# A mixture-of-experts routing table kept by expert and rank, written while tokens are still being counted

## The chip, the core and the metric

The kernel runs on one core of one Trainium2 chip. The metric is the device time of one execution in microseconds. A core has TensorE (PE), VectorE (DVE), ScalarE (ACT), GpSimd (POOL) and SyncE (SP), which run side by side, each through its own list of instructions in order. SP and POOL also issue DMA transfers; the indirect ones (rows picked by a list of indices) are POOL's.

## What is computed

8192 tokens of 512 numbers are first modulated per batch (a product with a 512x512 matrix), then go through a shared expert and through 8 of 64 routed experts, and the sum is added to the input. Cut to what matters here:

```python
x, cond_512: (8, 1024, 512), (8, 256)
y = clip(((x * styles) @ weight.T) * dcoefs + bias, -256, 256)        # 8192 tokens
shared = silu(y @ sh_gate_w) * (y @ sh_up_w) @ sh_down_w               # hidden width 1024
scores = sigmoid(y @ router_w.T); sb = scores + e_bias                 # 64 experts in 8 groups of 8
# the 4 groups with the largest sum of their two best sb stay; of them the 8 best experts
topk_idx = top_k(where(in 4 groups, sb, -inf), 8); w = scores[topk_idx] / (sum + 1e-20)
order = argsort(topk_idx.reshape(-1), stable=True)                     # 65536 (token, expert) pairs
tok = order // 8
o = (silu(y[tok] @ gate_w[e]) * (y[tok] @ up_w[e])) @ down_w[e]        # expert of each pair, width 256
routed[tok] += o * w
out = x + shared + routed
```

How many tokens an expert gets depends on the data.

## The kernel before

All products are made from high and low halves of the float32 numbers, three matmuls for each.

*Stage one* (to about 244 us) goes over 16 tiles of 512 tokens: load_x brings a tile of x on SP, split_x makes its halves (ACT xh, DVE xl), cond multiplies on PE, cond_out and cond_lo make y, its halves, its transposed copy for DRAM (y_d by rows, yT_d by columns), logits and scores make the router's scores. early_masks makes the first MA = 2 of eight masks meanwhile: route_mask(c) marks, for chunk c of 1024 tokens, the 8 chosen experts of every token, on DVE alone.

*Stage two* (to about 1343 us) is the shared expert: 128 steps, 8 for each tile of 512 tokens. A step is gate_up (24 matmuls), hidden (ACT, DVE, ACT, DVE) and the down products of the step before (12 matmuls), about 8.2 us. The order of PE, ACT, DVE and SP is written out by hand. Between the steps runs the generator route_slots, which makes the routing table on DVE. Each step has a credit of DVE time (the last lines of the loop) and takes pieces of the generator until the credit is used; HOP ends the step's share, because a matmul that was put into the list "later" has to run first, behind the next gate_up.

The table (tokw) says for every block of 128 places which token and which weight each place has. A block belongs to one expert; blocks are processed in units of one, two or four, of which there are fixed numbers (64, 64, 85, and up to 15 more of four, in groups that are skipped if not wanted). Before: the remaining masks, sums per chunk (r8), totals per expert, the layout of units, and then for each chunk ranks and slots (count, raise_), the eight largest (V.max), their scores (q, w8), the weights, and the address ad. Then POOL writes the chunk's 8 x 8 columns of 128 pairs (token, weight), 8 bytes a pair, with 64 indirect transfers to the table's copy in DRAM, tab_d; every burst of 8 of them waits until the burst before has landed. After the last chunk one transfer reads tab_d back to tokw.

At step 124 the first weights and the first gathers of *stage three* are put into the order, and from step 126 its first transposes; stage three goes over the 213 units: gather of rows of y_d by tokw (POOL), turn_x (PE), halves (ACT xh, DVE xl), gate and up (part, half), down_c, weigh, and scatter, an indirect transfer that adds to out (POOL). Its order comes from plan and arrange, a small scheduler at build time.

Of the kernel before, what the change touches and what calls it, by code (L numbers as in the profile page):

```python
# [21 lines left out]
P = 128  # L22
B, L, C = 8, 1024, 512
N = B * L
# [39 lines left out]
def body(ctx, tc, xT, x, condT, wT, vecs, affT, rwT, ebias, wexp, shgu, shdn, cst, out):  # L64
# [12 lines left out]
    tab_d = nc.dram_tensor("tab_d", [P * NSB, 2], I32).ap()  # L77
# [8 lines left out]
    tokw = pp.tile([P, NSB, 2], I32, name="tokw")  # L86
# [64 lines left out]
    MA = 2  # L151
    GUA = (1, 2, 13)
    rank0 = rp.tile([P, NBC, G, G], F32, name="rank0")
    V.memset(rank0, 0.0)
# [49 lines left out]
    with ExitStack() as actx:  # L204
# [167 lines left out]

        with tc.manual_schedule(engines={ET.PE, ET.Activation, ET.DVE}):
# [20 lines left out]
            for j in range(1, NT):  # L394
# [3 lines left out]
                if j in GUA:  # L398
                    fetch_gu(GUA.index(j), xa, 1)
                for m in range(KC):  # L400
                    cond_to(j, m)
                    for k in range(KC):
                        cond(j, m, k)
                    for k in ((0,), (1,), (), (2, 3))[m] if more else ():
                        split_x(j + 1, k)
                    cond_out(j, m)
                    cond_lo(j - (m == 0), (m - 1) % KC)
                    if m == 1 and j >= 2:
                        scores(j - 2)
                    elif j >= 3 and m % 2 == 0:  # L410
                        next(mgen, None)
# [71 lines left out]
    def gather(u, s, g):  # L483
        queued(GP.indirect_dma_start(xg[g % RXG].bitcast(F32), None, y_d, IOA(tokw[:, u.block + s, 0:1], 0)))  # L484
# [49 lines left out]
    def weigh(u, s, d):  # L534
        S.mul(oc[d % ROC], po[d % 2], tokw[:, u.block + s, 1:2].bitcast(F32))  # L535

    def scatter(u, s, d):
        i_ = queued(GP.indirect_dma_start(out, IOA(tokw[:, u.block + s, 0:1], 0), oc[d % ROC], None, compute_op=ALU.add))  # L538
# [205 lines left out]
    with ExitStack() as bctx:  # L744
# [19 lines left out]
        def route_slots():  # L764

            for c in range(MA, NB // NBC):
                for cost in route_mask(c):
                    yield cost  # L770

            for c in range(NB // NBC):
                V.tensor_reduce(r8[:, :, c], mask[:, c].bitcast(F32), axis=AX.X, op=ALU.add)
                yield 0.8
            rs = sbt.tile([P, E, NB // NBC], F32R, name="rs", tag="d2")
            V.tensor_tensor_scan(rs.rearrange("p e c -> p (e c)"), rst, r8.rearrange("p e c -> p (e c)"), 0.0, ALU.mult, ALU.add)
            ps = psr.tile([P, 512], F32, name="ps")
            later.append(lambda: PE.matmul(ps, lhsT=oner, rhs=rs.rearrange("p e c -> p (e c)"), start=True, stop=True))
            yield HOP
            base = sbt.tile([P, E, NB // NBC], F32, name="base", tag="dd")  # L780
            V.tensor_copy(base, ps.rearrange("p (e c) -> p e c", e=E))


            ecnt = sbt.tile([E, 12], F32, name="ecnt")
            eci = sbt.tile([E, 4], I32, name="eci")
            ed = sbt.tile([E, E], F32, name="ed")
            V.tensor_tensor(ed, base[:E, :, NB // NBC - 1], ident[:E, :E], ALU.mult)
# [18 lines left out]
            tb = sbt.tile([P, 2, 8], I32, name="tb")  # L806
            gp = sbt.tile([P, 8], F32, name="gp")
            gs = sbt.tile([P, 8], F32, name="gs")
# [11 lines left out]
            off = 0  # L820
            for b in range(TBITS - 1, -1, -1):
                V.tensor_scalar(tbit[:, b:b + 1], ti[:, 5:6], b, 1, ALU.logical_shift_right, ALU.bitwise_and)
                V.tensor_scalar(tb[:, 0, b:b + 1], ti[:, 5:6], b + 1, b + 1, ALU.logical_shift_right, ALU.logical_shift_left)
                V.tensor_scalar(tb[:, 1, b:b + 1], tb[:, 0, b:b + 1], -4.0, 4.0 * off, ALU.mult, ALU.add)
                off += 1 << b
            yield 1.5
            V.tensor_copy(gp[:, :TBITS], tb[:, 0, :TBITS])
            V.tensor_tensor(gs[:, :TBITS], tb[:, 1, :TBITS], tbit[:, :TBITS], ALU.mult)
# [13 lines left out]

            dg = sbt.tile([E, 5, E], F32, name="dg", tag="d2")
            e6 = sbt.tile([E, 8], F32, name="e6")
            V.tensor_scalar(e6[:, 1:2], ecnt[:, 4:5], float(P), None, ALU.mult)
            V.scalar_tensor_tensor(e6[:, 0:1], ecnt[:, 1:2], -float(QT), e6[:, 1:2], ALU.mult, ALU.add)
            V.scalar_tensor_tensor(e6[:, 2:3], ecnt[:, 2:3], -2.0, ecnt[:, 5:6], ALU.mult, ALU.add)
            V.scalar_tensor_tensor(e6[:, 2:3], e6[:, 2:3], float(P), e6[:, 1:2], ALU.mult, ALU.subtract)
            V.scalar_tensor_tensor(e6[:, 3:4], ecnt[:, 2:3], 2.0 * P, e6[:, 1:2], ALU.mult, ALU.add)
            V.tensor_tensor(e6[:, 4:5], ecnt[:, 6:7], ecnt[:, 3:4], ALU.subtract)  # L850
            V.tensor_tensor(e6[:, 4:5], e6[:, 4:5], ecnt[:, 5:6], ALU.subtract)
            V.tensor_scalar(e6[:, 4:5], e6[:, 4:5], float(P), None, ALU.mult)
            for q in range(5):
                V.tensor_scalar(dg[:, q], ident[:E, :E], e6[:, q:q + 1], None, ALU.mult)
            later.append(lambda: PE.matmul(ps[:, 192:192 + 5 * E], lhsT=ones[:E], rhs=dg.rearrange("p a e -> p (a e)"), start=True, stop=True))

            def count(c):
                so = sbt.tile([P, E, 8], F32R, name="so", tag="d2")
                V.tensor_tensor_scan(so.rearrange("p e b -> p (e b)"), rst, mask[:, c].rearrange("p e b -> p (e b)").bitcast(F32), 0.0, ALU.mult, ALU.add)

                def over():
                    PE.matmul(ps, lhsT=oner, rhs=so.rearrange("p e b -> p (e b)"), start=True, stop=False)
                    PE.matmul(ps, lhsT=trir, rhs=mask[:, c].rearrange("p e b -> p (e b)"), start=False, stop=True)

                later.append(over)

            def raise_(c):
                sc = rp.tile([P, E, 8], F32, name="sc", tag="sb")
                V.tensor_tensor(sc, ps.rearrange("p (e b) -> p e b", b=8), first[:, :, c:c + 1].to_broadcast([P, E, 8]), ALU.add)  # L873
                yield 0.8

                dd = sbt.tile([P, E, 8], F32, name="dd")
                d2 = sbt.tile([P, E, 8], F32, name="d2")
                for d_, o_ in ((dd, 1), (d2, 3)):
                    V.tensor_tensor(d_, sc, odd[:, o_].unsqueeze(2).to_broadcast([P, E, 8]), ALU.is_gt)
                    V.tensor_tensor(d_, d_, odd[:, o_ + 1].unsqueeze(2).to_broadcast([P, E, 8]), ALU.mult)  # L880
                    yield 1.5
                V.tensor_tensor(dd, dd, d2, ALU.add)
                V.tensor_tensor(sc, sc, dd, ALU.add)
                V.tensor_tensor(sc, sc, mask[:, c].bitcast(F32), ALU.mult)
                yield 2.1
                return sc

            yield HOP
            odd = sbt.tile([P, 5, E], F32, name="odd")
            V.tensor_copy(odd, ps[:, 192:192 + 5 * E].rearrange("p (a e) -> p a e", e=E))  # L890
            first = sbt.tile([P, E, NB // NBC], F32, name="first")
            V.tensor_copy(first[:, :, 0], odd[:, 0])
            V.tensor_tensor(first[:, :, 1:], base[:, :, :-1], odd[:, 0].unsqueeze(2).to_broadcast([P, E, NB // NBC - 1]), ALU.add)
            count(0)
            yield HOP

            def owners():

                ic = sbt.tile([E, NE], F32, name="ic", tag="d2")
                for o, blk in ((0, cs[:E, C_IOTA:C_GRP]), (NE - NX, ex)):  # L900
                    q = ic[:, o:o + blk.shape[-1]]
                    V.tensor_scalar(q, blk, ecnt[:, 4:5], None, ALU.is_ge)
                    V.scalar_tensor_tensor(q, blk, ecnt[:, 5:6], q, ALU.is_ge, ALU.add)
                    V.scalar_tensor_tensor(q, blk, ecnt[:, 6:7], q, ALU.is_ge, ALU.add)
                later.append(lambda: PE.matmul(ps[:1, 192:192 + NE], lhsT=ones[:E, 0:1], rhs=ic, start=True, stop=True))
                yield HOP
                ie = sbt.tile([1, 2, NE], F32, name="ie", tag="dd")
                V.tensor_scalar(ie[:, 0], ps[:1, 192:192 + NE], E - 0.5, -float(E), ALU.is_gt, ALU.mult)
                V.tensor_tensor(ie[:, 1], ie[:, 0], ps[:1, 192:192 + NE], ALU.add)
                V.tensor_scalar(ie[:, 0], ie[:, 1], E - 0.5, -float(E), ALU.is_gt, ALU.mult)  # L910
                V.tensor_tensor(ie[:, 1], ie[:, 0], ie[:, 1], ALU.add)
                V.tensor_scalar(iexp, ie[:, 1], float(E - 1), None, ALU.min)
                yield 1.5
# [3 lines left out]
            for c in range(NB // 8):  # L917
# [3 lines left out]
                if c == 1:  # L921
                    yield from owners()
# [252 lines left out]
```

## Time and profile before

| what | value |
|---|---|
| median of 3 runs | 3781.26 us (3776.44 to 3785.31) |
| profiled execution, its own time | 3782.01 us |
| its span, from the first to the last instruction | 3780.1 us |
| PE, DVE, ACT, POOL busy | 98%, 59%, 50%, 55% of the span |
| mean granted PE clock | 0.995 |
| table writes tab_d (L967), POOL | 512, mean 1045 ns |
| gathers xg (L484) and scatters out (L538), POOL | 532 each, mean 1121 and 1785 ns |

A profile row gives the start and the length of an instruction in microseconds, its engine, its line in the kernel and the tiles that it writes and reads; in brackets stands how long its engine was idle before it, and what ended that. Matmuls overlap, so their lengths add up to more than the time that they take; the distance of their starts says how fast they follow each other. SPq and POOLq are the engines' issuing parts.

### The profile page before, as it was taken

How to read it: one execution, taken by the hardware profiler on the slowest of the kernel's cores; microseconds unless marked ns; L12 is line 12 of the kernel's file. 1: busy time of each engine (PE TensorE's matmuls, PEld its weight loads, DVE VectorE, ACT ScalarE, POOL GpSimd, SP SyncE). 2: the span in 40 equal slices, each digit the busy share in tenths (PEclk: the TensorE clock that was granted, in tenths of full speed). 3: DMA queues.
4: the chain of work that ended last, by engine and by line, in shares of the span. 5: the costliest groups of instructions: out<-in, count | busy, mean ns of one | idle time of the engine just before them, and what ended most of it. 6: DMA issues, size and time to landing. Idle time of an engine off the chain costs nothing.

```text
span 3780.1 us, 53475 instructions
## 1 busy us (share of the span) xinstructions
PE 3720.7 (98%) x19009; PEld 3116.9 (82%) x19009; DVE 2240.5 (59%) x3429; ACT 1883.2 (50%) x2883; POOL 2089.8 (55%) x1588
## 2 busy tenths in 40 slices
PE   9999999999999899999999999999999999999998
PEld 7777778888888778888888888888888888888886
DVE  6778765666532255566656565656665656665654
ACT  6552111111111156666666666666666666666664
POOL 0000056666666656666666666666665666666663
PEclk9999999999999999999999999999999999999999
DMA  7751111112111277787776766776766676666664
GB/s 246 211 167 60 48 51 51 52 37 65 35 51 51 77 196 168 151 208 178 162 167 146 167 133 140 157 137 129 161 130 127 137 133 116 138 112 118 115 118 65
DMA packets 233333, 464.13 MB, mean 123 GB/s; under 512 B 42464, under 2 KB 75232, under 8 KB 227296
## 3 DMA queue, kind: packets, MB, share of 16 engines
q0 software_dynamic: 135696, 280.15, 40.2%
q1 hardware_dynamic: 96368, 179.40, 15.1%
q8 instruction: 152, 2.49, 0.3%
q14 instruction: 125, 1.02, 0.1%
q10 hardware_dynamic: 992, 1.06, 0.1%
HBM read 532.75 MB, written 191.97 MB: 192 GB/s over the span
## 4 chain that ended last, share of the span: by engine, by line
PE 83%; DVE 5%; POOL 5%; issue 3%; DMA 3%; ACT 1%; SPq 0%; POOLq 0%; DVEq 0%; ACTq 0%
PE pg L511 35%; PE po L531 20%; PE gu L116 11%; PE po L1017 5%; PE pg L520 5%; POOL tab_d L967 4%; PE pt L488 4%; PE py L305 2%; DMA tab_d<-tokw,ad 1%; DVE e L196 0%; DVE yl L69 0%; DMA yT_d<-yf 0%; PE pg L525 0%; DMA xr<-in_xT 0%; PE plt L330 0%
## 5 line engine op out<-in xcount | busy, mean ns | idle before, releaser
L538 POOL DMA_INDIRECT out<-oc,tokw x532 | 949.9, 1785 | 564.4 <-ACT oc L535 243.7
L967 POOL DMA_INDIRECT tab_d<-tokw,ad x512 | 534.9, 1045 | 742.0 <-DVE sc L873 451.1
L511 PE MATMUL pg<-xh,gh 128*128 128x512 f32 (+1 forms) x2384 | 834.1, 350 | 0.0
L511 PE MATMUL pg<-xh,gl 128*128 128x512 f32 (+1 forms) x2384 | 823.5, 345 | 0.0
L511 PE MATMUL pg<-xl,gh 128*128 128x512 f32 (+1 forms) x2384 | 820.8, 344 | 0.0
L484 POOL DMA_INDIRECT xg<-y_d,tokw x532 | 596.5, 1121 | 345.1 <-PE pt L488 194.9
L69 DVE TENSOR_TENSOR gl<-wg,gh 128x1024 fp32r<-128x1024 f32 x426 | 520.1, 1223 | 109.3 <-ACT gh L499 96.9
L511 PEld LDWEIGHTS pg<-xh,gl 128*128 128x128 f32 x2384 | 449.7, 189 | 57.1
L511 PEld LDWEIGHTS pg<-xl,gh 128*128 128x128 f32 x2384 | 449.8, 189 | 55.6
L511 PEld LDWEIGHTS pg<-xh,gh 128*128 128x128 f32 x2384 | 449.8, 189 | 53.1
L499 ACT CAST gh<-wg 128x1024 fp32r<-128x1024 f32 x426 | 448.1, 1055 | 0.7 <-DMA wg<-in_wexp 0.7
L535 ACT ACTIVATE oc<-po,tokw 128x512 f32<-128x512 f32 x532 | 369.5, 695 | 153.7 <-PE po L531 138.1
L69 DVE TENSOR_TENSOR xl<-pt,xh 128x512 fp32r<-128x512 f32 x532 | 357.0, 687 | 149.2 <-ACT xh L491 107.5
L531 PE MATMUL po<-dh,hh 128*128 128x512 f32 x1064 | 427.0, 401 | 1.0 <-ACT hh L660 1.0
L531 PE MATMUL po<-dh,hl 128*128 128x512 f32 x1064 | 418.4, 393 | 0.4 <-DVE hl L69 0.4
L531 PE MATMUL po<-dl,hh 128*128 128x512 f32 x1064 | 416.0, 391 | 0.0
L116 PE MATMUL gu<-yl,guh 128*128 128x512 f32 x1024 | 404.9, 395 | 4.4 <-DVE yl L69 4.4
L116 PE MATMUL gu<-yh,guh 128*128 128x512 f32 x1024 | 402.8, 393 | 3.9 <-ACT yh L72 3.9
L658 DVE TENSOR_TENSOR hf<-hf,pg 128x512 f32<-128x512 f32 x170 | 117.0, 688 | 481.4 <-PE pg L511 477.0
L116 PE MATMUL gu<-yh,gul 128*128 128x512 f32 x1024 | 401.5, 392 | 0.0
L491 ACT CAST xh<-pt 128x512 fp32r<-128x512 f32 x532 | 301.4, 587 | 189.4 <-PE pt L488 80.0
L69 DVE TENSOR_TENSOR dl<-wd,dh 128x1024 fp32r<-128x1024 f32 x213 | 260.6, 1224 | 89.4 <-ACT dh L499 72.9
(239 smaller groups left out, 5632.4 us busy)
## 6 DMA issues: line engine op xcount, KB each, us to landing
wg<-in_wexp SPq DMA_DIRECT2D x213, 1024.0 KB
wd<-in_wexp SPq DMA_DIRECT2D x213, 512.0 KB
y_d<-yt SPq DMA_DIRECT2D x64, 256.0 KB
xn<-in_x SPq DMA_DIRECT2D x64, 256.0 KB
out<-xn SPq DMA_DIRECT2D x64, 256.0 KB
xr<-in_xT SPq DMA_DIRECT2D x60, 256.0 KB
yT_d<-yf SPq DMA_DIRECT2D x60, 256.0 KB
yr<-yT_d SPq DMA_DIRECT2D x60, 256.0 KB
```

What stands on the lines that cost most here:

```text
L69: V.tensor_tensor(o, a, b, ALU.subtract)
L116: PE.matmul(p_, lhsT=w_[:, q * KC + k], rhs=y_[k], start=n == 0, stop=n == 3 * KC - 1)
L484: queued(GP.indirect_dma_start(xg[g % RXG].bitcast(F32), None, y_d, IOA(tokw[:, u.block + s, 0:1], 0)))
L491: S.copy(xh[u.xq][:, :, s * P:(s + 1) * P], pt_of(g).bitcast(F32))
L499: S.copy(a[u.q][:, sl], (wg, wg, wd)[c][u.kind][:, sl])
L511: PE.matmul(out, lhsT=w_[u.q][:, c:c + P], rhs=x_[u.xq][:, k, :w], start=n == 0, stop=n == 3 * KC - 1)
L520: PE.matmul(out.rearrange("p (o h) -> p o h", o=2), lhsT=x_[u.xq][:, k, :P], rhs=wv[:, k], start=n == 0 and i == 0, stop=n == 5 and i == 1)
L531: PE.matmul(po[d % 2], lhsT=h_[u.q][:, k, s * P:(s + 1) * P], rhs=w_[u.q][:, k * C:(k + 1) * C], start=n == 0, stop=n == 5)
L535: S.mul(oc[d % ROC], po[d % 2], tokw[:, u.block + s, 1:2].bitcast(F32))
L538: i_ = queued(GP.indirect_dma_start(out, IOA(tokw[:, u.block + s, 0:1], 0), oc[d % ROC], None, compute_op=ALU.add))
L967: i_ = GP.indirect_dma_start(tab_d, IOA(ad[:, b, k:k + 1], 0), tw[:, b, k], None)
L1017: PE.matmul(acc[j][s], lhsT=h_[:, ts], rhs=w_[c], start=c == 0 and n == 0, stop=c == HC - 1 and n == 2)
```

## The change

The table in DRAM gets a place for every expert and rank: 64 rows of 128 places for each of 64 experts, and four rows that stay empty. A pair's place is then expert x 8192 + rank, which needs no totals, so each chunk is written as soon as its mask and running counts are there. After the last chunk the totals are made, the layout of units follows as before, and for each of the 592 blocks the row of tab_d that belongs to it is computed. Five indirect reads fetch these rows (up to 128 of 1 KB each), and PE turns them into tokw (token and weight now lie in two halves of it). MA is 1. The credit is 2.7 in all steps. The empty table is written in four parts of 1 MB during tiles 3 to 6 of stage one. The generator waits, when the reads are issued, until step 118.

```diff
-    tab_d = nc.dram_tensor("tab_d", [P * NSB, 2], I32).ap()
+    NR = N // P
+    tab_d = nc.dram_tensor("tab_d", [E * NR + 4, 2 * P], F32).ap()
+    places = tab_d.rearrange("r (s w) -> (r s) w", w=2)
...
-    tokw = pp.tile([P, NSB, 2], I32, name="tokw")
+    tokw = pp.tile([P, 2 * NSB], F32, name="tokw")
+    slot_tok, slot_w = tokw[:, :NSB].bitcast(I32), tokw[:, NSB:]
...
-    MA = 2
+    MA = 1
...
+        pat = tokw[:, :2 * N * K // P]
+        tok = pat.rearrange("p (s w) -> p w s", w=2)[:, 0]
+        GP.memset(pat, 0.0)
+        GP.iota(tok.bitcast(I32), pattern=[[1, N * K // P]], base=N, channel_multiplier=0)
+        ini = wa.tile([P, 256], I32, name="ini")
+        GP.iota(ini[:, :P], pattern=[[1, P]], base=0, channel_multiplier=0)
...
+        def constants():
+            V.tensor_copy(tok, tok.bitcast(I32))
+            V.tensor_copy(ebase, ini[:, P:P + E])
+            V.tensor_copy(erow, ini[:E, 200:201])
+            V.tensor_copy(block, ini[:, :P])
...
+        def clear(r):
+            SP.dma_start(
+                tab_d[:E * NR].rearrange("(p r f) w -> p r (f w)", p=P, f=4)[:, 2 * r:2 * r + 2],
+                pat.unsqueeze(1).to_broadcast([P, 2, 8 * P]),
+            )
+            if r == 0:
+                SP.dma_start(tab_d[E * NR:].rearrange("(a r) w -> a (r w)", a=1), pat[0:1])
...
+                if j == 2:
+                    V.tensor_copy(tok, tok.bitcast(I32))
+                if 3 <= j < 7:
+                    clear(j - 3)
+                if j == 8:
+                    GP.iota(tok.bitcast(I32).rearrange("p (b k) -> p b k", k=K), pattern=[[P, NB], [0, K]], base=0, channel_multiplier=1)
+                if j == 10:
+                    constants()
...
 route_slots:
-            for c in range(MA, NB // NBC):
-                for cost in route_mask(c):
-                    yield cost
             for c in range(NB // NBC):
-                V.tensor_reduce(r8[:, :, c], mask[:, c].bitcast(F32), axis=AX.X, op=ALU.add)
-                yield 0.8
...
+                if c >= MA:
+                    yield from route_mask(c)
+                so = sbt.tile([P, E, 8], F32R, name="so")
+                d1 = sbt.tile([P, E, 8], F32, name="d1")
+                S.copy(d1, mask[:, c].bitcast(F32))
+                if c:
+                    V.tensor_tensor(d1[:, :, 0], d1[:, :, 0], upto.bitcast(F32), ALU.add)
+                V.tensor_tensor_scan(so.rearrange("p e b -> p (e b)"), rst, d1.rearrange("p e b -> p (e b)"), 0.0, ALU.mult, ALU.add)
+                upto = sbt.tile([P, E], F32R, name="upto", bufs=2)
+                V.tensor_copy(upto, so[:, :, 7].bitcast(F32))
+                def over():
+                    PE.matmul(ps, lhsT=oner, rhs=so.rearrange("p e b -> p (e b)"), start=True, stop=False)
+                    PE.matmul(ps, lhsT=trir, rhs=mask[:, c].rearrange("p e b -> p (e b)"), start=False, stop=True)
+                later.append(over)
+                yield HOP
+                sc = rp.tile([P, E, 8], F32, name="sc", tag="sb")
+                V.tensor_tensor(sc, ps.rearrange("p (e b) -> p e b", b=8), ebase.unsqueeze(2).to_broadcast([P, E, 8]), ALU.add)
+                V.tensor_tensor(sc, sc, mask[:, c].bitcast(F32), ALU.mult)
...
+                V.tensor_scalar(ad, p8, -1.0, None, ALU.add)
...
-                        i_ = GP.indirect_dma_start(tab_d, IOA(ad[:, b, k:k + 1], 0), tw[:, b, k], None)
+                        i_ = GP.indirect_dma_start(places, IOA(ad[:, b, k:k + 1], 0), tw[:, b, k], None)
...
-            GP.dma_start(tokw, tab_d.rearrange("(p s) w -> p s w", p=P))
...
+            for g in range(0, NSB, P):
...
+                inn = sbt.tile([E, 3, P], F32, name="inn", tag="so")
...
+                def row(inn=inn, n=n, g=g // P):
+                    for r in range(3):
+                        PE.matmul(ps[:n, g:g + 1], lhsT=inn[:, r, :n], rhs=ones[:E, 0:1], start=r == 0, stop=r == 2)
+                later.append(row)
+                yield HOP
...
+            for g in range(NG):
+                n = min(P, NSB - g * P)
+                GP.indirect_dma_start(tg[g][:n], None, tab_d, IOA(rows_[:n, g:g + 1], 0))
+            while len(holding):
+                yield HOP
+            for dst, w in ((slot_tok, 0), (slot_w, 1)):
+                for a in range(0, NG, 4):
...
+                            PE.transpose(ps[:, (g - a) * P:(g - a) * P + n], tg[g][:n].rearrange("b (s w) -> b w s", w=2)[:, w], ident[:n, :n])
+                    later.append(turn)
+                    yield HOP
+                    V.tensor_copy(dst[:, a * P:a * P + w_], ps[:, :w_])
...
-        SP.dma_start(tab_d.rearrange("(p s) w -> p s w", p=P), tini)
...
+                if i == len(steps) - 10:
+                    holding.clear()
-                credit = min(credit, 0.0) + (0.0 if not i else 2.5 if writing else 3.4 if i < HC else 5.5)
+                credit = min(credit, 0.0) + (0.0 if not i else 2.7)
```

The removed lines that are not shown are raise_, owners, the 320-column broadcast of five numbers per expert (dg, L843 to L855) and the search for a slot's group (L951 to L958).

## The prediction

> **What bounds the kernel now.** The page comes first: its busy shares, then the slices, then the stretches of the windows view around every slice in which the PE is not full.
>
> ```profile
> PE 3720.7 (98%) x19009; PEld 3116.9 (82%) x19009; DVE 2240.5 (59%) x3429; ACT 1883.2 (50%) x2883; POOL 2089.8 (55%) x1588
> PE   9999999999999899999999999999999999999998
> ...
> POOL 0000056666666656666666666666665666666663
> ```
>
> The PE is the bound: 3720.7 of 3780.1 us, so at most 59 us of it are idle time. An edit gains only where it removes such idle time (or a lowered clock), and every PE instruction that it adds in stage two is paid in full. The one weak slice in the middle is the 14th. The windows view (us, busy time and count by engine, clock, DMA share, GB/s) shows stage two as full and one hole:
>
> ```profile
> 900.00:1000.00 100.00, 100.00 (x439) 82.14 (x438) 58.97 (x102) 19.00 (x32) 63.66 (x61) 1.00 0.18 49
> 1200.00:1300.00 100.00, 100.00 (x438) 81.93 (x438) 24.27 (x37) 16.82 (x28) 65.32 (x66) 1.00 0.15 43
> 1300.00:1400.00 100.00, 86.23 (x445) 71.38 (x444) 47.49 (x60) 44.23 (x66) 52.70 (x45) 0.95 0.66 197
> ```
>
> The POOL and PE timelines tell what the hole is (start, length, what, and in brackets the idle time before it and its releaser):
>
> ```profile
> 483.21 1.46 POOL L967 DMA_INDIRECT tab_d<-tokw,ad  x1 [451.12 <-DVE sc L873]
> ...
> 1308.05 0.96 POOL L967 DMA_INDIRECT tab_d<-tokw,ad  x1 [0.31 <-issue]
> 1310.77 0.58 POOL L979 DMA_DIRECT2D tokw<-tab_d  x1 [1.76 <-DMA tab_d<-tokw,ad]
> 1319.57 1.01 POOL L484 DMA_INDIRECT xg<-y_d,tokw  x1 [8.22 <-DMA tokw<-tab_d]
> ...
> 1325.51 0.72 PE L488 MATMUL pt<-idr,xg 128*128 128x128 f32 x4 [12.06 <-DMA xg<-y_d,tokw]
> ```
>
> The 512 table writes hold POOL from 483 to 1309 us. The table is read back by 1319, the first gather lands at 1325.4, and the transposes that PE has in its order since 1313.45 wait 12.06 us. The time is set by when writing begins (483, at the end of step 24 of 128) and by its pace. The rest of the idle time stands in the PE's waits of two other stretches:
>
> ```profile
> PE py L305 <- DVE xl L289: 6.5, 6, 1.4
> PE py L305 <- ACT xh L288: 4.1, 4, 1.6
> ...
> 390.93 0.79 PE L116 MATMUL gu<-yl,guh 128*128 128x512 f32 x1 [3.29 <-DVE yl L69]
> 391.52 0.63 PE L116 MATMUL gu<-yh,gul 128*128 128x512 f32 x1
> ```
>
> The first two lines are stage one (60 to 240 us). At 390.93 the PE starts a tile of the shared expert late, because DVE is still in masks; and a wait has a second price: the next matmuls start 0.43 us apart instead of 0.23 until 397.0, 14 of them, 2.8 us more. The same holds at 318.93 (3.61 us of waiting for yh) and, shorter, after 1325.5.
>
> **The change part by part.**
>
> *Writing begins earlier.* A chunk's addresses no longer need all eight masks, the totals and the blocks. Counting out the new order of DVE's instructions by step gives addresses at the ends of steps 9, 21, 33, ... 93: twelve steps of about 8.2 us, 98 us a chunk. In before step 9 lies at about 335 us; with what is lost ahead of it I take 340. The pace of POOL: 512 writes from 483.2 to 1309 are 825 us, 1.61 each (mean 1.045 of generating, 0.30 of issue, and once in eight about 2.4 us of waiting for the burst before to land: (136.0 + 13)/63). 103 us a chunk is slower than DVE's 98, so POOL keeps the pace: the last write at 340 + 825 = 1165, landed at 1167. The blocks' rows are ready at step 103 (about 1120), the five reads of 1 KB rows stand behind the writes on POOL (and the gathers behind them), are issued at 1.0 us each and landed by about 1176. PE's transposes of them come at step 119, which the PE reaches at about 1256. The spare time is 89 us, 1.4 us for each of 63 burst waits.
>
> So the wait at 1313 goes: 12.06 us, and the slow matmuls after it (six at 0.43 for 0.23, and the first transposes 0.72 for 0.46: 1.4). What is late next: the second transposes need the one pt buffer back, behind h, hh, gh, gl, xl on ACT and DVE. The same chain one step later took 4.4 us from the end of a gate_up and left PE 1.16 us idle; here 1.3. Net -12.2. The gathers, now free from step 122 (about 1285), have 28 us for the 5.8 us that one took.
>
> *A rule against it.* Row first: a write took 962 ns at the median and 1877 at most, and the rate is 61 in 100 us beside a DVE at 59% and 66 beside one at 24%. The Trainium skill, SBUF — State Buffer, section Who interferes with whom, says that DVE in a two-port mode and GpSimd shut each other out for a whole instruction, and tensor_scalar is one that can enter it. The change moves seven masks under the writes. By the rule each of its 0.64 us tensor_scalars could hold a write up, 5 us or so in all with the small ones; by the row the whole spread between busy and idle DVE is 8%, some 65 us if I took it all. Both fit into 89 us; I take 0 on the path.
>
> *The writes' places.* Neighbouring ranks of an expert were 592 x 8 B apart, and are now 8 B apart. No row of before shows landing times for that. Low end: a little faster, worth nothing, for POOL is off the path then. High end: the Trainium skill, DMA: Bandwidth & Descriptors, Specifications, says that under 512 B an SDMA engine reads, modifies and writes, and its Latency section gives 0.8 us as the least round trip to HBM. If the 16 or so neighbours of a burst (1024 places over 64 experts) had to take turns, that would be 13 us a burst for 2.4, an estimate: 63 x 10.6 - 89, a sum of +570. The 2.4 us row is nearest (the same 8 B writes by the same queue); I take 2.4 to 2.9 and no cost, and keep the high end as a rival.
>
> *DVE at the start of stage two.* Credit per step falls from 5.5 to 2.7 in steps 8 to 22. Steps 14 and 15 carry about 7 us of DVE work for 8.2 us of PE, so yl is in time at 390: -3.3 - 2.8 = -6.1. The wait at 318 stays: it hangs on the last dnl of step 6 (a buffer that SP needs for yr), behind DVE's routing work, 4.3 us in before and two triples q, q, w in after, 2 x (1.14 + 0.69 + 0.69) = 5.0: +0.8. The small waits at 463 to 486 (1.8 in all): -0.8.
>
> *PE's own work.* Added: five groups of three 64x128 f32 matmuls with one column. The nearest row, L799 (two passes, 0.31 us with its weight loads), gives 3 x 0.31 + 0.1 = 1.0 a group: 5.0. Ten f32 transposes at 0.12 (L525: two in 0.24) with four gaps of 0.15: 1.8. Removed: the 320-column broadcast L855 (423.56 to 424.38, 0.82), and L778 becomes shorter (0.1). The counting matmuls stay eight pairs. Net +5.9, between 4 and 7. DVE's new block work (steps 94 to 103) and the eight copies of masks on ACT (17 to 20% busy) lie beside a full PE; without that cover they would cost 15 and 5 us.
>
> *Stage one.* SP gets four clears of 1 MB and one row of 4 KB; the old 592 KB clear goes. 30 us at 312 to 314 GB/s make 3.3 us a clear; the share of the DMA engines is 0.70 to 0.80 from 75 to 135 us, where they fall, and would be 0.95. Behind each clear on SP stand y_d, yT_d and the next xr, for which split_x, and then PE, wait. But SP itself waits for yt at that place (30.5 us in 10 waits), which takes most of a clear. Bounds 0 and 13 (all four), I take +3. One mask of two (some 10 us of DVE) leaves tiles 9 to 15, where PE is idle for 4 us: -1 (0 to -3). The constants are two strided casts of 512 and a few small DVE operations, about 2.2 us: +0.5 (0 to 2). POOL's four more iotas lie before its first squares at 5.8 us, where POOL waits for wr.
>
> Sum: -12.2 - 6.1 + 0.8 - 0.8 + 5.9 + 3 - 1 + 0.5 = -9.9 us. The profiled execution had a span of 3780.1 and its own time was 3782.0, 1.9 around it; it stands 0.7 above the median 3781.3. The sum goes from 3782.0 to 3772.1, from the median to 3771.4.
>
> **The rivals.**
>
> *Landing becomes the bound* (slower). Adjacent 8 B places land later, and every burst of eight waits for the one before. It decides at 1.4 us more per burst, 3.8 instead of 2.4: from there PE stands at step 119, 63 us for each further us. At 4.5 that is 63 x 0.7 = 44 us, less the 9.9: 3815; break-even is at 3.95. For it: the wait is inside POOL's loop already, and single bursts took 5.0. Against: in before such bursts are few, and 1024 small writes in 12.9 us are a low rate. Chance 0.11.
>
> *Stage one pays more.* The engines are full from 75 to 135 us, latencies double (4.2 us for xr), and xr, yt and yf come late in a chain. Then +12 in place of +3, and PE's slow starts behind some waits: 3781, between 3777 and 3787. For it: SP's queue is in order, and xr is waited for already (15.7 us by ACT). Against: the gaps of 5 to 6 us on SP before y_d. Chance 0.18.
>
> *The hole stays.* Gathers or weights could be held by something else at the same place (memory of stage two's pools, SP's loads), so the early table brings nothing there: -9.9 + 12.2 = +2.3: 3783.7. Against: POOL's gather waited for tokw and nothing else, and the weights came 1 us after the last write let go of its addresses. Chance 0.06.
>
> **How the numbers follow.** The forecast has 0.65, on its own 3764 to 3779; 0.11, 0.18 and 0.06 are the rivals. 0.2% is 7.6 us, about what a measurement of this kernel can tell from no change: faster is below 3773.7, slower above 3788.8. The forecast lies 2 us inside; with the spread of its terms about 0.57 of all is faster, 0.26 same (the rest of the forecast, most of stage one's rival, the hole), 0.17 slower (landing, the upper tail of stage one, and a DVE that now runs late at chunk ends). The range 3760 to 3793 leaves out landing at full price and a few in a hundred below.
>
> **What would show it.** Right: first table write near 340, the last near 1165, five tg reads before 1180, no wait for xg at 1313, no wait at 390, PE's DVE- and ACT-waits of stage one within 5 us of 10.6. Wrong: a burst wait above 3.8 us; ps transposes of tg waiting for DMA; PE idle by over 8 us more between 75 and 135 us; more than 1 us per group of row matmuls.

## The result: 3% slower, and where the time went

| | before | after |
|---|---|---|
| median | 3778.56 us (3776.44 to 3785.31, 6 runs) | 3894.36 us (3892.86 to 3898.12, 6 runs) |
| ratio | | 1.0304 (95% interval 1.0291 to 1.0318) |
| span of the profiled execution | 3780.1 us | 3890.8 us |
| mean granted PE clock | 0.995 | 0.980 |
| first and last table write | 483.2, 1308.1 us | 335.2, 1364.3 us |

The forecast was 3771.4 us with a range of 3760 to 3793. The page of the changed kernel has PE and POOL as follows (busy time and share, then the span in 40 slices):

```profile
PE 3722.7 (96%) x19047; PEld 3120.7 (80%) x19047; DVE 2197.2 (56%) x3336; ACT 1888.8 (49%) x2891; POOL 2091.0 (54%) x1596
...
PE   9999999999998089999999999999999999999998
...
POOL 0002555544544526666666656666566666666663
```

PE is busy for 2 us more than before. What is new is a slice with no PE work at all, the 14th. POOL now begins in the fourth slice instead of the sixth, and works at a lower share. The windows view (us, busy time and count by engine, clock, DMA share, GB/s) around it:

```profile
900.00:1000.00 100.00, 100.00 (x437) 81.81 (x436) 62.68 (x133) 19.14 (x33) 50.31 (x48) 1.00 0.36 63
...
1200.00:1300.00 100.00, 46.66 (x205) 38.12 (x204) 10.77 (x16) 9.49 (x16) 47.95 (x50) 0.75 0.10 22
1300.00:1400.00 100.00, 25.35 (x103) 20.02 (x104) 6.68 (x11) 2.44 (x4) 49.26 (x52) 0.60 0.18 54
```

POOL issues 48 writes in the 100 us from 900, where before it issued 61. From 1246 to 1372 PE does nothing, and the granted clock falls with it. The timelines of POOL and PE:

```profile
335.15 1.17 POOL L870 DMA_INDIRECT tab_d<-tokw,ad  x1 [220.72 <-DVE sb L170]
...
1364.34 0.96 POOL L870 DMA_INDIRECT tab_d<-tokw,ad  x1 [0.30 <-issue]
1369.55 0.98 POOL L1000 DMA_INDIRECT tg<-tab_d,rows__9258  x1 [4.25 <-DMA tab_d<-tokw,ad]
...
1377.61 0.96 POOL L533 DMA_INDIRECT xg<-y_d,tokw  x1 [2.11 <-DVE tokw L1015]
```

```profile
1372.37 0.49 PE L1011 MATMUL ps<-cs,tg 128*128 128x128 f32 x1 [125.71 <-DMA tg<-tab_d,rows__9258]
```

Writing began 148 us earlier than before and ended 56 us later. PE's transposes of the fetched rows, at step 119, stood 125.7 us behind the first of five reads, which stood behind the last write. The waits of POOL show what made the writes slow (line, releaser: us in all, times, longest), before and then after:

```profile
POOL tab_d L967 <- DMA tab_d<-tokw,ad: 136.0, 58, 5.0
```

```profile
POOL tab_d L870 <- DMA tab_d<-tokw,ad: 337.7, 62, 10.7
```

A burst of eight now keeps POOL waiting 5.4 us for its landing (337.7/62), where before it was 2.3 (136.0/58). The writes themselves did not become longer (mean 1020 ns, before 1045). From the first write to the last it is 2.01 us for each, before 1.61: (1364.3 - 335.2)/511.

It is not for lack of bandwidth. Two of the waits are 9.66 us up to 869.0 and 5.84 us up to 884.6. The first had other traffic beside it (DMA share 0.68 from 859.4 to 869.0). Around the second the DMA engines did next to nothing (share 0.01), and it stood all the same:

```profile
868.00:888.00 20.00, 20.00 (x89) 16.51 (x88) 11.81 (x22) 3.06 (x5) 10.41 (x11) 1.00 0.01 1
```

```profile
869.01 0.96 POOL L870 DMA_INDIRECT tab_d<-tokw,ad  x1 [9.66 <-DMA tab_d<-tokw,ad]
884.65 0.95 POOL L870 DMA_INDIRECT tab_d<-tokw,ad  x1 [5.84 <-DMA tab_d<-tokw,ad]
```

The trace's own records of DMA packets show where the time lies. The 512 writes leave 8192 packets of 64 B in both kernels, of 19 ns each in the mean in both. What grew comes after them: from the start of a burst's last such packet to the end of POOL's wait it is 4.0 us in the changed kernel (mean of its 57 waits of over 1 us) and 1.3 us before (56 waits). Other traffic lengthens a wait (6.8 us in the mean, against 4.9 in the 27 waits with a DMA share under 0.05), but not this part of it: 4.0 us against 4.1.

### The profile page after: what moved, and what is told of

Read it like the earlier page. It is cut to its first block, busy times and chain, and to the rows that moved or that the text cites. A ratio compares the mean times of both kernels' runs of the same rounds, so it can differ in the third digit from the quotient of the medians.

```text
span 3890.8 us, 53491 instructions
## 1 busy us (share of the span) xinstructions
PE 3722.7 (96%) x19047; PEld 3120.7 (80%) x19047; DVE 2197.2 (56%) x3336; ACT 1888.8 (49%) x2891; POOL 2091.0 (54%) x1596
## 4 chain that ended last, share of the span: by engine, by line
PE 85%; DMA 5%; POOL 4%; issue 2%; DVE 2%; ACT 1%; POOLq 0%; SPq 0%; DVEq 0%; ACTq 0%
PE pg L560 34%; PE po L580 19%; PE gu L121 13%; PE po L1045 7%; PE pg L569 5%; POOL tab_d L870 4%; PE pt L537 4%; DMA tab_d<-tokw,ad 4%; PE py L315 3%; DMA xr<-in_xT 1%; PE pg L574 0%; PE plt L340 0%; DVE xl L299 0%; DVE yl L69 0%; ACT yf L321 0%
## 5 line engine op out<-in xcount | busy, mean ns | idle before, releaser
L870 POOL DMA_INDIRECT tab_d<-tokw,ad x512 | 522.5, 1020 | 728.4 <-DMA tab_d<-tokw,ad 337.7
L560 PEld LDWEIGHTS pg<-xl,gh 128*128 128x128 f32 x2384 | 449.8, 189 | 55.7
L131 ACT ACTIVATE h<-gu 128x512 f32<-128x512 f32 x128 | 76.5, 597 | 546.3 <-PE gu L121 536.4
```

Of the source, the lines that this page charges most:

```text
L560: PE.matmul(out, lhsT=w_[u.q][:, c:c + P], rhs=x_[u.xq][:, k, :w], start=n == 0, stop=n == 3 * KC - 1)
L870: i_ = GP.indirect_dma_start(places, IOA(ad[:, b, k:k + 1], 0), tw[:, b, k], None)
```

## The experiments

Three things about the places are new: neighbouring ranks are 8 B apart instead of 4736 (NEAR); the experts' rows begin 64 KB apart, a power of two (PITCH); and the table reaches over 4 MB instead of 0.6 (RANGE). "Burst wait" below is POOL's waiting for the landing of its own table writes, in all, divided by the number of waits that the view counts. (Bursts of eight leave 63 such waits; the view counts 57 to 69 of them in the table below, so a difference of 0.2 us in it says nothing.) Experiment 1 has four runs, each of the others one, which is the profiled one.

**1. Ranks 64 B apart in the same row.** A permutation inside each row of 128 places, with five small DVE instructions more for each chunk:

```diff
                 V.tensor_scalar(ad, p8, -1.0, None, ALU.add)
+                V.tensor_scalar(t1, ad, 15, 3, ALU.bitwise_and, ALU.logical_shift_left)
+                V.tensor_scalar(t2, ad, 4, 7, ALU.logical_shift_right, ALU.bitwise_and)
+                V.tensor_scalar(ad, ad, 7, 7, ALU.logical_shift_right, ALU.logical_shift_left)
+                V.tensor_tensor(t1, t1, t2, ALU.add)
+                V.tensor_tensor(ad, ad, t1, ALU.add)
```

> After, with the places permuted inside each row of 128 (1 KB): rank r goes to place 8*(r mod 16) + (r/16 mod 8), so that neighbouring ranks lie 64 B apart instead of 8 B. The row of a block and the set of its tokens stay. Theory NEAR (writes of a burst that fall into one small stretch of DRAM are taken in turn, and the stretch is 64 B or less): the wait per burst falls from 5.7 us to 2.4 to 3, a write to 1.6 to 1.7 us, last write near 1170, time 3765 to 3780. NEAR with a stretch of 512 B or more: no change, 3894. Theory PITCH (the experts' 64 KB pitch puts equal ranks on one channel) and theory RANGE (4 MB instead of 0.6 MB are written to): no change, 3894.

Measured: 3761.72 us, ratio 0.995 (0.9933 to 0.9966) to the kernel before. The wait of POOL:

```profile
POOL tab_d L877 <- DMA tab_d<-tokw,ad: 169.2, 65, 5.3
```

2.6 us for a burst, the last write at 1199.1, and no wait of PE for tg. Rows, pitch and reach of the table are those of the changed kernel, so the distance between neighbours is the cause. This version is faster than both kernels, than the one before by 0.5%.

**2. Ranks 512 B apart.** The same with other shifts, which mix the rows of an expert, so that the routed part of the output is not the right one; the instructions and their number stay.

```diff
-                V.tensor_scalar(t1, ad, 15, 3, ALU.bitwise_and, ALU.logical_shift_left)
-                V.tensor_scalar(t2, ad, 4, 7, ALU.logical_shift_right, ALU.bitwise_and)
-                V.tensor_scalar(ad, ad, 7, 7, ALU.logical_shift_right, ALU.logical_shift_left)
+                V.tensor_scalar(t1, ad, P - 1, 6, ALU.bitwise_and, ALU.logical_shift_left)
+                V.tensor_scalar(t2, ad, 7, 63, ALU.logical_shift_right, ALU.bitwise_and)
+                V.tensor_scalar(ad, ad, 13, 13, ALU.logical_shift_right, ALU.logical_shift_left)
```

> After, with rank r of an expert written to place 64*(r mod 128) + r/128 of its 8192 places: neighbouring ranks 512 B apart. This puts pairs into rows of other blocks, so the routed part is computed with mixed-up tokens; the number and kinds of instructions, blocks and units stay. NEAR, whatever the stretch up to 512 B: 1.6 us a write, last write near 1165, time about 3770. PITCH and RANGE (pitch and range are those of after): 2.0 us a write, 3894.

Measured: 3763.12 us; writes from 336.7 to 1163.0, 1.62 each, which is the pace of before.

```profile
POOL tab_d L877 <- DMA tab_d<-tokw,ad: 146.8, 57, 5.6
```

That is 2.6 us each. Beyond 64 B there is little left to gain.

**3. Another pitch.** 72 rows for an expert instead of 64, so that experts begin 72 KB apart; neighbours stay at 8 B.

```diff
-    NR = N // P
+    NR = N // P + 8
```

> After, with 72 rows per expert instead of 64 (a pitch of 72 KB; one of the four clears grows by half a MB). PITCH: the wait per burst falls to about 2.4 us, time about 3772. NEAR and RANGE: 2.0 us a write as in after, 3894 (3 us more at the most for the clear).

Measured: 3910.66 us, the last write at 1382.8.

```profile
POOL tab_d L870 <- DMA tab_d<-tokw,ad: 372.9, 62, 14.6
```

The waits are no shorter, 6.0 us each, and experiment 1 was fast at the old pitch. PITCH falls.

**4. Near places in the kernel before.** Its 512 writes go to a second table of the old size, where the places of a block are neighbours. The table that is read back stays empty, so the routed part of the output is left out; the instructions of before stay.

```diff
+    near_d = nc.dram_tensor("near_d", [P * NSB, 2], I32).ap()
-                V.scalar_tensor_tensor(ad, lo, float(NSB), si, ALU.mult, ALU.add)
+                V.scalar_tensor_tensor(ad, si, float(P), lo, ALU.mult, ALU.add)
-                        i_ = GP.indirect_dma_start(tab_d, IOA(ad[:, b, k:k + 1], 0), tw[:, b, k], None)
+                        i_ = GP.indirect_dma_start(near_d, IOA(ad[:, b, k:k + 1], 0), tw[:, b, k], None)
```

> Before, with only the places of its 512 writes changed: block*128 + (rank mod 128), 8 B apart for neighbouring ranks, in a second table of the same 0.6 MB; tokw is read from the first table, so all pairs are empty ones and the routed part is left out of the output, with the same instructions. NEAR: a write takes about 2.0 us instead of 1.61, the last one comes near 1510, and the hole at the start of stage three grows by some 200 us: about 3980. PITCH and RANGE (no 64 KB pitch, the same 0.6 MB): 1.61 us a write as in before, 3779.

Measured: 3954.49 us. The waits of POOL and of PE:

```profile
POOL near_d L968 <- DMA near_d<-tokw,ad: 324.1, 65, 12.3
```

```profile
PE pt L489 <- DMA xg<-y_d,tokw: 134.7, 1, 134.7
```

5.0 us for a burst and 1.94 us for a write, in a table of 0.6 MB: near places are enough, without any other part of the change. RANGE falls.

The wait for xg grew by 122.6 us, the span by 172.5. The other 49 us were lost before, between steps 80 and 107: DVE had to wait until a buffer of the addresses (ad, three of them) was given back by the late writes, and PE then waited for hh, which hangs on DVE (36.6 us up to 1129.8).

```profile
DVE ad L953 <- DMA near_d<-tokw,ad: 57.1, 2, 43.9
```

**5. Longer bursts, near places.** The changed kernel with `BURST = 16` for 8.

> The changed kernel with bursts of 16 writes instead of 8, so 31 waits for landing instead of 63; the places stay neighbours. Turns (every write takes about 2.0 us to land, because its places fall into the same small stretches as those of the writes beside it): the waits are half as many and twice as long, 10 to 11 us, the last write is again near 1364 us, PE waits over 110 us for tg, about 3894 us. Delay (a burst's last writes land some 3 us later than before, whatever number is in flight): waits stay near 5.5 us, 31 x 3 = 93 us less than 63 of them, the last write before 1210 us, no wait for tg, about 3763 us.

Measured: 3818.11 us; the last write at 1188.1; no wait for tg.

```profile
POOL tab_d L870 <- DMA tab_d<-tokw,ad: 150.3, 31, 9.7
```

It is 4.85 us for each wait. So the wait belongs to the burst, not to the write: with twice the number in flight it is no longer. "Turns", as it was put there, falls. But the time is 55 us above the 3763 that "Delay" gave, because of something that neither named. PE stopped in the middle of gate_up, with no releaser in the trace, here in part while POOL waited for a burst:

```profile
580.50 0.49 PE L121 MATMUL gu<-yh,gul 128*128 128x512 f32 x1 [2.31 <-issue]
581.90 0.59 PE L121 MATMUL gu<-yh,guh 128*128 128x512 f32 x1 [0.91 <-issue]
```

```profile
583.24 0.96 POOL L870 DMA_INDIRECT tab_d<-tokw,ad  x1 [3.89 <-DMA tab_d<-tokw,ad]
```

Such stops ("issue") come 23 times at this line, 20.5 us in all (31 times and 25.5 us with PE's other lines), and matmuls behind them follow at the slower pace, some 15 us more; ACT and DVE idled through the same stretch. Between steps 24 and 107, by the starts of each step's h on DVE, this kernel lost 65.8 us against before, and the changed kernel 9.1. (The 47 us that the expectation of experiment 9 names is how late step 107 is, with the gain ahead of step 24 set against the loss.) Stops and slower matmuls make 41 of the difference of 57, PE's waits for DVE and ACT another 7.7.

**6, 7. Ranks 16 B and 32 B apart.** As in 1, with `63, 1` and `6, 1`, and with `31, 2` and `5, 3`, in the first two lines.

> The changed kernel with the 128 places of a row permuted so that neighbouring ranks lie 16 B apart (rank r at place (r and 63) x 2 + (r >> 6)): of the 16 or so neighbours of a burst four share an aligned stretch of 64 B, where the changed kernel has eight and the layout with 64 B one. If the stretch that is taken in turn is 64 B: burst waits between the two, near 4 us, last write near 1270, PE waits some 30 us for tg or just not, 3765 to 3800 us. If it is 16 B or less: waits as with 64 B (2.6 us), last write near 1200, 3762 us. If it is 128 B or more, the 64 B layout would already share it with two or more, and this one lies nearer to the changed kernel: above 4.5 us a burst.

> The same with neighbouring ranks 32 B apart (rank r at place (r and 31) x 4 + (r >> 5)): two neighbours share 64 B. If the stretch is 64 B: burst waits a little above the 2.6 us of the 64 B layout, 3 to 3.4, last write near 1220, 3762 us. If it is 32 B or less: 2.6 us, last write 1199. If it is 128 B or more: 3.5 us and above.

Measured: 3773.12 and 3761.48 us.

```profile
POOL tab_d L877 <- DMA tab_d<-tokw,ad: 242.4, 65, 8.6
```

```profile
POOL tab_d L877 <- DMA tab_d<-tokw,ad: 173.2, 69, 6.9
```

With 16 B it is 3.7 us for a burst (the last write at 1247.1, just behind PE's step 119, which waits 9.4 us for tg), with 32 B 2.5 us, no more than with 64. All of it in one table:

| neighbours apart | places in 32 B | burst wait, us | us for each write |
|---|---|---|---|
| 8 B (after) | 4 | 5.4 | 2.01 |
| 16 B | 2 | 3.7 | 1.79 |
| 32 B | 1 | 2.5 | 1.68 |
| 64 B | 1 | 2.6 | 1.69 |
| 512 B | 1 | 2.6 | 1.62 |
| 4736 B (before) | 1 | 2.3 | 1.61 |

About 1 us for each further place in the same 32 B fits the first three rows. That the limit is an aligned stretch of 32 B, and not how densely places lie, isn't separated by these runs.

**8. The credit of before in the first steps**, on the 64 B layout:

```diff
-                credit = min(credit, 0.0) + (0.0 if not i else 2.7)
+                credit = min(credit, 0.0) + (0.0 if not i else 3.4 if i < HC else 5.5 if i < 23 else 2.7)
```

> The layout with 64 B between neighbours, and the credit of DVE time of the kernel before in the first steps: 3.4 in steps 1 to 7, 5.5 in steps 8 to 22, then 2.7 as in the changed kernel. The prediction put 6.1 us on the wait at 390 us, the changed kernel showed about 8 us between steps 8 and 16 and 7 more up to step 30. If the credit is the cause: the DVE wait of PE near 390 is back, PE's steps 16 to 30 begin 6 to 13 us later than in the 64 B layout with credit 2.7, about 3771 us; writing begins earlier, near 315 us. If it is another part (the masks' place, the removed per-chunk sums and layout), the steps begin within 2 us of the 64 B layout, about 3762 us.

Measured: 3786.99 us. From step 0 to step 30 it loses 23.4 us to the 64 B layout, more than either side gave. The wait at 390 comes back (2.15 us at 399), but most of it is a wait that neither kernel has: the ranks' matmul, put behind a gate_up, now stands before DVE's scan is done, three times, 14.3 us:

```profile
349.51 0.80 PE L837 MATMUL ps<-so,oner 128*128 128x512 f32 x1 [5.80 <-DVE so L832]
```

Writing began at 329.2, not near 315. So the low credit is a part of the change that the early writing can't do without.

**9. Bursts of 16 with 32 B between neighbours.**

> The layout with 32 B between neighbours, and bursts of 16. With neighbours and bursts of 16 the burst waits halved in number (31 of 4.85 us), but PE, DVE and POOL stood still together at some 20 moments without a releaser in the trace, and PE lost about 47 us between steps 24 and 107. In flight (16 writes of 128 pairs outstanding are the cause, whatever their places): the same moments again, 20 to 60 us lost, about 3790 to 3820 us. Near places (a long queue only together with places that share 32 B): none of them, burst waits of 2.5 us 31 times, last write near 1110, about 3761 us.

Measured: 3762.45 us; the last write at 1120.3, 1.53 us for each write; not one PE stop without a releaser in stage two.

```profile
POOL tab_d L877 <- DMA tab_d<-tokw,ad: 70.6, 35, 4.7
```

The waits are 2.0 us each. The changed kernel, near places with bursts of 8, has no such stop either: by these single runs the stops of 5 need both, near places and a long burst.

**10. Two masks in stage one** (`MA = 2` on the 64 B layout).

> The layout with 64 B, and two masks instead of one in stage one (MA = 2, as in the kernel before). The prediction: the second mask costs 1 us of PE in stage one (0 to 3), so the first step of stage two begins 1 us later than the 252.9 us of the 64 B layout; writing does not begin earlier, since the first chunk needs one mask alone; the second chunk's mask is gone from stage two, some 10 us of DVE. If early stage two depends on DVE's work alone, steps 8 to 16 gain up to 2 us. About 3761 to 3764 us.

Measured: 3764.57 us; the first step of stage two begins at 258.2. Nine kernels with one mask and the same stage one began it at 252.8 to 257.0, mean 254.3, so the second mask costs about 4 us, with a spread as large; 1 was assumed. The kernel before has two masks as well, and began at 253.7: what is 4.5 us later here are the clears and the constants, again no more than the spread. Steps 0 to 30 gain 16.9 us against before, the 64 B layout 16.1: under 1 us.

**11. The clears issued twice** (the line `clear(j - 3)` repeated, on the 64 B layout).

> The layout with 64 B, and each of the four clears of 1 MB issued twice. The prediction took 3 us for four clears (0 to 13). If that size is right, four more cost 3 us or more: the first step of stage two begins near 256 to 260 us, about 3766 us. If SP's own wait takes them (it waits for yt at that place), the first step stays within 1 us of 252.9, about 3762 us.

Measured: 3774.81 us; the first step begins at 267.4, 13.1 us behind the mean of those nine kernels (14.5 behind the 64 B layout). So four more clears cost about 3.3 us each, which is the whole time of a transfer as the prediction had it; SP's own wait does not take them.

**12. Bursts of 4, near places** (`BURST = 4` in the changed kernel).

> The changed kernel with bursts of 4 writes, neighbours 8 B apart. Burst waits so far: 5.4 us with four places in 32 B, 3.7 with two, 2.5 with one, and 4.85 with four and bursts of 16. Stretch (the delay is about 1 us for each further place in the same 32 B, whatever the length of the burst; 8 neighbours of a burst of 4 still fill stretches): 127 waits of 5 to 5.5 us, 10.5 us for 4 writes, last write near 1680 us, about 4210 us. Burst (the delay grows with the neighbours in the burst, half as many here): waits of 3.9 us, last write near 1500, about 4030 us.

Measured: 4075.52 us; waits 555.9 us in 123, 4.5 each; the last write at 1547.2.

```profile
POOL tab_d L870 <- DMA tab_d<-tokw,ad: 555.9, 123, 8.6
```

The time lies between the two expectations, and so does the wait: 4.5, 5.4 and 4.85 us for bursts of 4, 8 and 16. The wait depends little on the length of the burst, and that it rises from 4 to 8 and then not is left open. As in 4, slow writes also reached DVE and PE before the table was wanted: DVE waited for a buffer of the addresses, PE then for DVE (53.2 us up to 1108.8), and 77 us were lost between steps 24 and 107.

```profile
DVE ad L866 <- DMA tab_d<-tokw,ad: 80.5, 2, 61.7
```

## Why the prediction was wrong

**The step that failed is "the writes' places".** It bounded the landing from 2.4 to about 13 us a burst, took "2.4 to 2.9 and no cost", and kept the upper end as a rival with a chance of 0.11. It measured 5.4 us. The choice followed "the nearest row", the same 8 B writes by the same queue. But that row shared with the new writes everything except the one property that the edit changed, the distance between places, and so it could not tell anything of it. The argument against, that 1024 small writes in 12.9 us are a low rate, was true and beside the point: the DMA share was 0.01 around a wait that stood all the same, and the extra time came after the DMA engines' packets.

The upper end was wrong too. It took a burst's 16 neighbours as waiting for one another, after the section Specifications of the Trainium skill's DMA: Bandwidth & Descriptors (under 512 B an SDMA engine reads, modifies and writes). All rows of the table above are writes of 8 B, and neighbours at 32 B lie 16 to a stretch of 512 B, at 2.5 us a burst: what is paid for here are places within some 32 B of each other.

**The rival had the rule right.** It put the point of decision at 3.8 us and the price at 63 us for each further us: 63 x (5.4 - 3.8) = 101, with the sum of -9.9 that is 3873. Measured are 21 us more. PE was at step 119 at 1246 and not 1256, since more was saved ahead of it than the sum had; and the remaining difference lies in the pace: the last write would be at 340 + 825 + 63 x (5.4 - 2.4) = 1354 and was at 1364. The two other rivals did not come: stage one lost 0.3 us, and the hole at 1313 went.

**The sum of the other steps.** The starts of each step's h on DVE (L127 before, L132 after) give what each stretch gained, and the idle time and slower matmuls of PE within it give the terms:

| step of the sum, us | predicted | after | 64 B layout |
|---|---|---|---|
| stage one (clears, mask, constants) | +2.5 | +0.3 | -0.8 |
| wait near 318 | +0.8 | -3.7 | -4.3 |
| wait at 390 | -6.1 | -6.3 | -6.3 |
| waits at 463 to 486 | -0.8 | -3.0 | -3.0 |
| PE's own work | +5.9 | +5.6 | +5.6 |
| wait for xg at 1313 | -12.2 | -12.3 | -12.3 |
| wait for tg at step 119 | 0 | +130.7 | 0 |
| sum; difference of the spans | -9.9 | 111.3; 110.7 | -21.1; -21.4 |

- *The hole at 1313* was right to 0.1 us, by itself: the same step gains 12.3 in the changed kernel and in the 64 B layout.
- *PE's own work*: +6.3 in steps 93 to 107 (some 1.9 of it matmuls that before has in steps 17 to 30), +1.2 for the transposes (1.8 assumed).
- *The wait at 390* was right with both its parts, 3.29 and 2.8. The same second price, slower matmuls behind every wait, was not put on the three small ones: 1.8 of waiting, 1.2 of slower matmuls.
- *The wait near 318* was expected to grow and shrank. PE before, then after:

```profile
318.93 0.79 PE L116 MATMUL gu<-yh,guh 128*128 128x512 f32 x1 [3.61 <-ACT yh L72]
```

```profile
317.17 0.54 PE L121 MATMUL gu<-yh,guh 128*128 128x512 f32 x1 [2.64 <-ACT yh L72]
```

  It was counted from the DVE work of the generator alone (5.0 for 4.3). With the neighbouring wait for yl (0.74) down to 0.19 and fewer slow matmuls (9 for 18) it is 3.7 us better. Why DVE is earlier there by this much wasn't tried by itself.
- *Stage one*: +2.5 lies within what kernels with the same stage one show among themselves, -0.9 to +3.3. Its parts can't be told apart from that spread: by experiment 10 clears and constants cost about 4.5 (3.5 assumed) and the mask is worth about 4 (1 assumed), so that the two nearly cancel. Between 75 and 135 us, where the clears fall, PE was busy 1.9 us less than before (53.8 for 55.7, at a DMA share of 0.87 for 0.75).
- *DVE beside the writes* was taken as 0, and is: a write takes 1015 to 1048 ns in all these kernels.

So the reasons for a gain held, and more than held: 21 us of span in the 64 B layout, 0.5% by its runs. The changed kernel gave them back six times over at one place that was counted as nothing. With the places 32 or 64 B apart, the change does what it says.

## What to carry to other kernels

When an edit moves where small writes land, the row of the old writes is no evidence for the new ones, however alike the instructions are; bound the landing from both ends, and if a queue waits for landings burst by burst, multiply the unknown by the number of bursts before choosing an end. Keep records that are written by indirect transfers at about the same time apart; in this kernel 32 B were enough, and a permutation inside the row cost five small instructions a chunk. The reader need not undo it where, as here, the order within a block doesn't matter. A scheme that starts early needs the pace of its slowest queue, not only its start: here 148 us of lead were used up by 3 us a burst.

## What the runs showed of the hardware that was not expected

- Eight-byte writes whose places share 32 B land later: 5.4 us for a burst of eight writes of 128, against 2.3 to 2.6 us at 32 B and more, and the extra time lies after the DMA engines' packets (4.0 us from the last one to the end of the wait, against 1.3), with other traffic or without.
- With 16 such writes in flight PE stopped 23 times within gate_up, 20.5 us in all, without a releaser; with places 32 B apart it did not stop once (one run of each). The pages of both list DMA queues called instruction (152 and 124 or 125 packets), and a load of instructions held up with the writes would look like this; that was not tried by itself.
- Four transfers of 1 MB more, eight for four, cost about 13 us in a stage whose DMA share was 0.87 already where they fall, 3.3 us each. What the first four cost can't be told from the stage's spread of 4 us.
